# An RWKV block with FP4 feed-forward: small loads packed into one array, the decay's two chunks side by side, levels 0 and 1 in one burst, and the last feed-forward tiles split into two chunk streams

## The chip, the cores and the metric

The kernel runs on one core of a Trainium2 chip. The core has five engines that take their instructions in order, each from its own queue: TensorE (PE, matrix products; PEld is its weight load), VectorE (DVE), ScalarE (ACT), GpSimd (POOL) and SyncE (SP, which here only issues DMAs). The metric is the device time of one execution in microseconds (us). Lower is better.

## The reference

The input `x` is (2, 4096, 256): two sequences of 4096 tokens with 256 channels. Two small networks are joined by modulation with six vectors that come from a condition `c`:

```python
sa, ca, ga, sb, cb, gb = split(silu(c) @ wmod)
h = layernorm(x) * (1 + ca) + sa
x = x + ga * rwkv(h)                      # two layers, then a layernorm
h = layernorm(x) * (1 + cb) + sb
x = x + gb * fp4_linear(silu(fp4_linear(h, w_gate)) * fp4_linear(h, w_up), w_down)
```

A layer of `rwkv` has a time mix and a channel mix. The time mix shifts the sequence by one token, makes five mixtures of `x` and the shift (w, k, v, r, g) through two small products `tm_w1`, `tm_w2`, projects them to r, k, v, g, and makes a decay `w = exp(-exp(time_decay + tanh(wx @ td_w1) @ td_w2))` per token and channel. Four heads of 64 channels then run a recurrence over all 4096 tokens:

```python
out_t  = r_t @ (S + u * k_t v_t^T)
S      = S * w_t + k_t v_t^T
```

`fp4_linear` rounds its input and its weight, in blocks of 16, to the eight magnitudes of a four-bit float and multiplies. The feed-forward is 256 to 704 to 256. All arithmetic is float32.

## The kernel before

A tile is 256 tokens of one sequence, held as two chunks (C = 2) of 128 tokens. There are 2 sequences, 16 tiles each, and 2 layers, so the recurrence `wkv` is run 64 times; I call each run a round. A round does not step token by token. It builds, for each chunk, the 128 by 128 products of queries and keys in seven levels: level `l` holds pairs of tokens that lie in neighbouring halves of a block of `2 * 2**l` tokens. Before each next level DVE multiplies r and k (`upd`) by the decay over the half block, so that level l+1 needs the update of level l. Level 0 reads its own copies `r0`, `k0`, in which ACT has put the bonus `u`, so it does not need the update. The pair products are many small matmuls of 64 rows by 32 columns that write the PSUM tile `pa`. A lock (`head_lock`) lets one round at a time use `pa`, `diag`, `attn` and the state `S`.

The feed-forward (`ffns`) takes a finished tile, normalises it, rounds it to FP4 (`fp4`), transposes it, and then handles chunk 0 and after it chunk 1: gate and up products in two halves, silu on ACT and DVE, `fp4` over 704 columns, six transposes, the down product with `wd`, the residual on POOL. `fp4` is eight DVE instructions and one on ACT, each of which needs the one before.

The order of the work is not written out by hand. The program records its operations through a planner, class `Plan`. Each stream (the first layer of each sequence, the second layer of each sequence, the feed-forward, the feed-forward's weights, the conditioning) is a Python generator that records operations until its queue is full; the planner repeatedly takes the operation that could start first by its own table of durations, and so fixes one static order for each engine. It keeps PSUM banks, work buffers (`slot`, `long`, `tiny`) and estimated ends. All recorded operations therefore carry one line number in the profile, L262, and are told apart by the names of their tiles. Only the loads at the start are recorded directly, at L485; SP issues them in the order in which they stand in its queue, each with a wait on one of eight counters that an earlier load must have raised.

Names that the prediction uses: `slot,td` on PE are the decay's two products (`td1` with 128 rows and 128 columns, `td2` with 64 rows and 128 columns); `pa` the pair products, with `slot,slot` for level 0 (its queries and keys lie in two tiles) and `slot` for the others; `kv` the state's product, 128 rows by 64 columns; `S` and `attn` the products that read the state and the pair matrix; `cWk`, `cWv`, `cWr` the channel mix; `wg`, `wu`, `wd` the feed-forward; `ident` a transpose; `scales` the block scales of `fp4`. In a shape such as `64*32` the profile gives the rows and columns of the array that a matmul uses, which I call its form. A float32 matmul shows as two instructions.

In `td1` the weight is stored twice side by side, so that one matmul over all 256 tokens leaves two copies of its 64 outputs in the 128 partitions; `td2` then takes output half j = 0 from the upper copy and j = 1 from the lower.

Of the kernel before, what the change touches and what calls it, by code (L numbers as in the profile page):

```python
# [37 lines left out]
TINY = 24  # L38
# [3 lines left out]
FFN_SHARE = 1.4  # L42
# [3 lines left out]
MAGIC = 1.5 * 2.0**22  # L46

# [7 lines left out]
    "L0_ffn_w_up", "L0_ffn_w_down", "L0_c", "L0_wmod",  # L55
]
# [47 lines left out]
class Plan:  # L104
# [174 lines left out]

    def run(self, streams, stock):  # L280
        streams = [Stream(*q) for q in streams]
        while True:
# [24 lines left out]
            if not can:  # L307
                assert all(st.gen is None and not st.queue for st in streams), "stuck"
                return
# [72 lines left out]
def rwkv_adaln_fp4_kernel(ctx: ExitStack, tc: tile.TileContext, a: dict, out: bass.AP):  # L382
# [74 lines left out]
    scales = wk.tile([P, 3 * (FI // QB)], F32, name="scales")  # L457
# [32 lines left out]
    with nc.allow_non_contiguous_dma(reason="two vectors of 256"):  # L490
        for b in range(B):
            load(cT[:, :, b], a["L0_c"][b].rearrange("(k p) -> p k", p=P))
# [12 lines left out]
    load(lnw[:1, :D], a["L0_attn_ln_out_w"].unsqueeze(0))  # L505

    def load_mat(name, src, kc):
# [5 lines left out]
    VECS = ["ln1_w", "ln2_w", "x_maa", "w_maa", "k_maa", "v_maa", "r_maa", "g_maa",  # L513
            "gn_w", "gn_b", "ck_maa", "cr_maa", "time_decay", "time_first"]
    lay = []
    for i in range(L):
        w = {}
        vec = const.tile([P, len(VECS), J], F32, name=f"vec{i}")
        for n, v in enumerate(VECS):
            src = a["L0_attn_" + v][i]  # L520
            if v.startswith("time"):
                src = src.rearrange("h k -> (h k)")
            with nc.allow_non_contiguous_dma(reason="a vector of 256"):
                load(vec[:, n, :], src.rearrange("(j p) -> p j", p=P))
            w[v] = vec[:, n, :]

        w1 = a["L0_attn_tm_w1"][i].rearrange("(k p) n -> p k n", p=P)
        w["w1"] = wp.tile([P, J, 8 * E], F32, name=f"w1_{i}")  # L530
        load(w["w1"][:, :, : 5 * E], w1)
        for m in range(5, 8):
            load(w["w1"][:, :, m * E : (m + 1) * E], w1[:, :, 4 * E :])
        w2 = a["L0_attn_tm_w2"][i].rearrange("f e d -> (f e) d")
        w2a = wp.tile([P, D], F32, name=f"w2a_{i}")
        load(w2a, w2[0:P, :])
        w2b = wp.tile([2 * E, D], F32, name=f"w2b_{i}")
        for m in range(2):
            load(w2b[m * E : (m + 1) * E, :], w2[P : 5 * E, :])
        w["w2"] = [w2a[E * f : E * (f + 1), :] for f in range(4)]  # L540
        w["w2b"] = w2b
        for n in ("Wr", "Wk", "Wv", "Wg", "Wo"):
            w[n] = load_mat(f"{n}_{i}", a["L0_attn_" + n][i], J)
        w["wvm"] = const.tile([P, J * H], F32, name=f"wvm{i}")
        w["centred"] = False
        w["td1"] = wp.tile([P, J, 2 * ED], F32, name=f"td1_{i}")
        w["td2"] = wp.tile([2 * ED, D], F32, name=f"td2_{i}")
        for m in range(2):
            load(
                w["td1"][:, :, m * ED : (m + 1) * ED],  # L550
                a["L0_attn_td_w1"][i].rearrange("(k p) n -> p k n", p=P),
            )
            load(w["td2"][m * ED : (m + 1) * ED, :], a["L0_attn_td_w2"][i])
        w["cWk"] = load_mat(f"cWk_{i}", a["L0_attn_cWk"][i], J)
        w["cWv"] = load_mat(f"cWv_{i}", a["L0_attn_cWv"][i], FD // P)
        w["cWr"] = load_mat(f"cWr_{i}", a["L0_attn_cWr"][i], J)
        lay.append(w)
        load_wmod(1 + i)
# [7 lines left out]
    def fp4(nc, src, n, rows, dst, st, y, p):  # L566
# [10 lines left out]

        def blk(t):
            return t[:rows, :n].rearrange("p (b q) -> p b q", q=QB)

        am, sc, inv = (st[:rows, m * (FI // QB) : m * (FI // QB) + nb] for m in range(3))
        sb = src.rearrange("p (b q) -> p b q", q=QB)
        nc.vector.tensor_reduce(am, sb, AX.X, ALU.max, apply_absolute_value=True)
# [4 lines left out]
        nc.vector.scalar_tensor_tensor(blk(y), sb, DOWN, invb, ALU.mult, ALU.mult)  # L588
        nc.vector.tensor_scalar(
            p[:rows, :n].bitcast(I32), y[:rows, :n].bitcast(I32), STEP_BITS, None, ALU.bitwise_and  # L590
        )
        yield
        yv, pv = y[:rows, :n], p[:rows, :n]
        nc.vector.scalar_tensor_tensor(yv, pv, MAGIC, yv, ALU.mult, ALU.add)
        nc.vector.scalar_tensor_tensor(yv, pv, -MAGIC, yv, ALU.mult, ALU.add)
        nc.scalar.activation(yv, yv, AF.Copy, bias=MAGIC)
        yield
        nc.vector.scalar_tensor_tensor(
            dst.rearrange("p (b q) -> p b q", q=QB), blk(y), MAGIC, scb, ALU.subtract, ALU.mult
        )  # L600
# [190 lines left out]
    def wkv(i, b, rk_s, dec_s, v_s):  # L791
# [20 lines left out]
        for l in range(7):  # L812
            h = 1 << l
# [17 lines left out]
            if l == 0:  # L831
                give(r0_s, k0_s)
# [94 lines left out]
    def time_mix(i, b, h):  # L927
# [62 lines left out]
        for k in range(J):  # L990
            mm(pd[:, 0:TT], w["td1"][:, k, :], xw[:, k, :], k == 0, k == J - 1)
        give(xw_s)
        td_s = take_slot()
        td = td_s[:, :TT]
        pl.scalar.activation(td, pd[:, 0:TT], AF.Tanh)
# [14 lines left out]
        for j in range(J):  # L1010
            js = slice(j * ED, (j + 1) * ED)
            mm(os[j][:, :TT], w["td2"][js, j * P : (j + 1) * P], td[js, :], True, True)
# [3 lines left out]
        for j in range(J):  # L1016
            pl.scalar.activation(
                dec[:, :, j, :], os[j][:, :TT].rearrange("p (c t) -> p c t", c=C), AF.Exp,
                bias=w["time_decay"][:, j : j + 1],
            )  # L1020
            pl.close(bks[j])
# [85 lines left out]
    def conditioning():  # L1107
# [5 lines left out]
        lnb_s, wide_s, tmp_s = take_slot(), take_slot(), take_slot()  # L1113
        lnb = lnb_s[:, :D]
# [3 lines left out]
        pl.gpsimd.partition_broadcast(lnb, lnw[:1, :D])  # L1118
# [25 lines left out]
        give(lnb_s, wide_s, tmp_s, lnw)  # L1144
        tiny.append(few)

    def ffn_weights():
# [3 lines left out]
        for src, dst in ((a["L0_ffn_w_gate"], wg), (a["L0_ffn_w_up"], wu)):  # L1151
            for n0 in range(0, FI, P):
                n = min(P, FI - n0)
                wt, y, p = (pl.take(long) for _ in range(3))
                pl.sync.dma_start(out=wt[:n, :D], in_=src[n0 : n0 + n, :])
                yield from fp4(pl, wt[:n, :D], D, n, wt[:n, :D], scales, y, p)
# [9 lines left out]
                long.extend((wt, y, p))  # L1166
                yield
        for m in range(J):
            wt, y, p = (pl.take(long) for _ in range(3))
            pl.sync.dma_start(out=wt[:, :FI], in_=a["L0_ffn_w_down"][m * P : (m + 1) * P, :])  # L1170
            yield from fp4(pl, wt[:, :FI], FI, P, wt[:, :FI], scales, y, p)
# [10 lines left out]
            long.extend((wt, y, p))  # L1182
# [62 lines left out]
    def ffns():  # L1245
        HF = FI // 2
        while "ffn" not in known:
            yield
        for _ in range(B * NT):
            while not done:  # L1250
                yield
# [5 lines left out]
            xf = xn.rearrange("p c d -> p (c d)")  # L1257
            y_s, p_s = pl.take(long), pl.take(long)
            yield from fp4(pl, xf, C * D, P, xf, scales, y_s, p_s)
            long.extend((y_s, p_s))  # L1260
# [5 lines left out]
            give(xn_s)  # L1266
            yield
            ob_s = take_slot()
            ob = v3(ob_s)
            for c in range(C):  # L1270
                cs_ = slice(c * P, (c + 1) * P)
                hb_s = pl.take(long)
                hb = hb_s[:, :FI]
                for s in range(2):
                    fs = slice(s * HF, (s + 1) * HF)
                    bk, gp = pl.bank()
                    for k in range(J):
                        mm(gp[:, :HF], xqT[:, k, cs_], wg[:, k, fs], k == 0, k == J - 1)
                    pl.scalar.activation(hb[:, fs], gp[:, :HF], AF.Sigmoid)
                    pl.vector.tensor_tensor(hb[:, fs], hb[:, fs], gp[:, :HF], ALU.mult)  # L1280
                    pl.close(bk)
                    yield
                    bk, up = pl.bank()
                    for k in range(J):
                        mm(up[:, :HF], xqT[:, k, cs_], wu[:, k, fs], k == 0, k == J - 1)
                    pl.vector.tensor_tensor(hb[:, fs], hb[:, fs], up[:, :HF], ALU.mult)
                    pl.close(bk)
                    yield
                y_s, p_s = pl.take(long), pl.take(long)
                yield from fp4(pl, hb, FI, P, hb, scales, y_s, p_s)  # L1290
                long.extend((y_s, p_s))
                hT_s = pl.take(long)
                hT = hT_s.rearrange("p (f n) -> p f n", f=NF)
                for g in range(2):
                    bk, pt = pl.bank()
                    for f in range(3):
                        at0 = f_at[3 * g + f]
                        tr(pt[:, f * P : (f + 1) * P], hb[:, at0 : at0 + P])
                    pl.scalar.copy(
                        hT[:, 3 * g : 3 * g + 3, :], pt[:, : 3 * P].rearrange("p (f n) -> p f n", f=3)  # L1300
                    )
                    pl.close(bk)
                    yield
                long.append(hb_s)
                bk, y = pl.bank()
                for f in range(NF):
# [39 lines left out]
```

## Time and profile before

| | |
|---|---|
| median of 3 runs | 3216.84 us (3215.44 to 3220.56) |
| the profiled execution | 3216.25 us, its span 3214.5 us |
| granted TensorE clock, mean | 0.970 |
| PE busy | 3034.9 us, 94% of the span |
| DVE busy | 2386.1 us, 74% |
| ACT busy | 1621.0 us, 50% |
| POOL busy | 937.6 us, 29% |

The 1.75 us between span and time lie outside the instructions. The shares are means over three stages that differ: a start in which PE does little, a long middle in which it hardly pauses, and an end in which only the feed-forward is left. A busy PE is counted from the modelled ends of its matmuls, so the start of one group to the start of the next is the better measure of what a group costs.

### The profile page before, as it was taken

The numbers are of one execution on the slowest core, as the hardware profiler recorded it, in microseconds if no ns is written. First come the engines' busy times: TensorE is split into PE (matmuls) and PEld (weight loads), VectorE is DVE, ScalarE is ACT, GpSimd is POOL, SyncE is SP. The second block draws the span as 40 slices with busy tenths as digits, with TensorE's granted clock in tenths as the row PEclk, the third lists the DMA queues.
The fourth block names the chain that finished last, engine by engine and source line by source line (L and its number), as shares of the span: only waits on it lengthen the run. The fifth ranks groups of instructions, "written<-read, shape, count | busy, mean of one in ns | idle before, by whom it ended". The sixth has DMA issues, their size and how long they took to land.

```text
span 3214.5 us, 88104 instructions
## 1 busy us (share of the span) xinstructions
PE 3034.9 (94%) x37948; PEld 2423.3 (75%) x37948; DVE 2386.1 (74%) x6146; ACT 1621.0 (50%) x3244; POOL 937.6 (29%) x857
## 2 busy tenths in 40 slices
PE   3899999999999999999999999999999999999875
PEld 2677778787777778788777777878787787778653
DVE  4687777787877777777777876787787787777764
ACT  1465554555555555555555454555554555554321
POOL 1233332232323333223223232233233233322210
PEclk7899999999999999999999999999999999999987
DMA  4000000000000000000000000000000000000000
GB/s 130 17 20 5 9 8 8 12 15 8 9 8 8 15 9 15 8 6 11 8 15 8 8 11 5 18 5 14 8 9 8 12 11 9 11 2 14 12 4 10
DMA packets 46856, 42.31 MB, mean 13 GB/s; under 512 B 13185, under 2 KB 44930, under 8 KB 46466
## 3 DMA queue, kind: packets, MB, share of 16 engines
q1 hardware_dynamic: 46466, 36.68, 3.8%
q8 instruction: 298, 4.88, 0.6%
q14 instruction: 92, 0.75, 0.1%
HBM read 28.28 MB, written 8.39 MB: 11 GB/s over the span
## 4 chain that ended last, share of the span: by engine, by line
PE 77%; DVE 10%; ACT 6%; issue 3%; POOL 1%; DMA 1%; SPq 1%; POOLq 0%; DVEq 0%; ACTq 0%
PE bank L262 69%; PE pa L262 7%; DVE slot L262 5%; ACT slot L262 3%; DVE long L262 2%; ACT attn L262 2%; DVE tiny L262 1%; PE kv L262 1%; DVE scales L262 1%; POOL slot L262 1%; SPq L485 1%; DVE diag L262 1%; ACT L262 1%; ACT long L262 1%; POOL tiny L262 0%
## 5 line engine op out<-in xcount | busy, mean ns | idle before, releaser
L262 POOL TENSOR_TENSOR slot<-slot,slot 128x512 f32<-128x512 f32 x416 | 503.5, 1224 | 980.0 <-DVE slot L262 692.5
L262 ACT ACTIVATE slot<-bank 128x512 f32<-128x512 f32 (+1 forms) x644 | 338.2, 530 | 692.7 <-PE bank L262 662.1
L262 POOL TENSOR_TENSOR tiny<-tiny,nhalf 128x2 f32<-128x2 f32 (+1 forms) x288 | 291.6, 1015 | 957.5 <-DVE tiny L262 867.3
L262 DVE TENSOR_TENSOR slot<-slot,slot 128x512 f32<-128x512 f32 x512 | 382.7, 749 | 102.4 <-PE pa L262 86.3
L262 PE MATMUL bank<-slot,cWk 128*128 128x256 f32 x1536 | 367.4, 385 | 2.8 <-DVE slot L262 1.7
L262 PE MATMUL bank<-cWv,slot 128*128 128x256 f32 x1536 | 344.1, 380 | 0.0
L262 PEld LDWEIGHTS pa<-slot 64*32 64x32 f32 x19456 | 222.1, 108 | 140.3 <-issue 54.6
L262 PEld LDWEIGHTS bank<-slot,cWk 128*128 128x128 f32 x1536 | 286.4, 191 | 45.7 <-DVE slot L262 2.8
L262 PEld LDWEIGHTS bank<-cWv,slot 128*128 128x128 f32 x1536 | 289.3, 190 | 39.6 <-ACT slot L262 0.3
L262 ACT ACTIVATE slot<-bank,vec 128x256 f32<-128x256 f32 x512 | 233.1, 496 | 154.2 <-PE bank L262 145.7
L262 DVE TENSOR_TENSOR slot<-slot,bank 128x512 f32<-128x512 f32 x192 | 131.0, 682 | 225.8 <-PE bank L262 203.6
L262 PE MATMUL pa<-slot 64*32 64x16 f32 x19456 | 264.2, 190 | 30.4 <-DVE slot L262 10.6
L262 DVE SCALAR_TENSOR_TENSOR slot<-bank,vec,slot 128x256 f32<-128x256 f32 x640 | 273.7, 473 | 18.8 <-PE bank L262 18.2
L262 POOL TENSOR_TENSOR slot<-slot 128x512 f32<-128x512 f32 x128 | 142.1, 1112 | 329.2 <-ACT slot L262 278.4
L262 DVE TENSOR_TENSOR long<-long,bank 128x352 f32<-128x352 f32 x256 | 131.8, 515 | 91.3 <-ACT long L262 67.6
L262 PE MATMUL bank<-ident,slot 128*128 128x128 f32 x1152 | 177.6, 282 | 23.1 <-ACT slot L262 15.9
L262 ACT ACTIVATE slot<-slot,tiny 128x256 f32<-128x256 f32 x256 | 142.1, 594 | 111.8 <-DVE tiny L262 90.3
L262 PE MATMUL bank<-wd,long 128*128 128x256 f32 x768 | 191.6, 402 | 0.2 <-ACT slot L262 0.2
L262 DVE SCALAR_TENSOR_TENSOR slot<-slot,vec,slot 128x256 f32<-128x256 f32 x384 | 179.3, 503 | 12.6 <-POOL slot L262 12.5
L262 ACT ACT_TABLE_LOAD x137 | 175.8, 1283 | 19.2 <-PE bank L262 9.5
L262 ACT COPY slot<-bank 128x512 f32<-128x512 f32 x224 | 130.0, 583 | 103.5 <-PE bank L262 99.5
L262 PE MATMUL bank<-wg,slot 128*128 128x352 f32 x512 | 177.8, 470 | 4.1 <-ACT slot L262 4.1
(112 smaller groups left out, 5796.3 us busy)
## 6 DMA issues: line engine op xcount, KB each, us to landing
slot<-in_L_attn_x_dram SPq DMA_DIRECT2D x64, 256.0 KB, 2.7
out_dram<-slot SPq DMA_DIRECT2D x32, 256.0 KB, 2.2
slot<-in_L_wmod_dram SPq DMA_DIRECT2D x6, 256.0 KB, 6.7
cWk<-in_L_attn_cWk_dram SPq DMA_DIRECT2D x2, 768.0 KB, 5.9
cWv<-in_L_attn_cWv_dram SPq DMA_DIRECT2D x2, 768.0 KB, 6.6
long<-in_L_ffn_w_down_dram SPq DMA_DIRECT2D x2, 352.0 KB, 2.8
long<-in_L_ffn_w_gate_dram SPq DMA_DIRECT2D x5, 128.0 KB, 4.9
long<-in_L_ffn_w_up_dram SPq DMA_DIRECT2D x5, 128.0 KB, 2.0
```

What stands on the lines that cost most here:

```text
L262: fn(*[real(v) for v in a], **{n: real(v) for n, v in k.items()})
L485: nc.sync.dma_start(out=dst, in_=src)
```

## The change

Four things are changed together.

1. **Loads.** Fourteen vectors, `tm_w1` (with its last part repeated), `tm_w2`, `td_w1` and `td_w2` of a layer came by 25 DMAs a layer. They are now laid out ahead of the launch as one array `small` of 128 by 1436, loaded by one DMA a layer; `cT` comes by one instead of two, and `ln_out_w` is loaded to all 128 partitions, where POOL's `partition_broadcast` spread it before.
2. **Decay.** `td_w1` is stored once. Its product is taken by chunk: chunk 0 to partitions 0 to 63, chunk 1 to 64 to 127, each with 128 rows by 64 columns and 128 tokens. `td2` uses row group c for chunk c, four products of 128 tokens for two of 256. The tanh works on 128 columns for 256, the first exponential on four pieces of 128 for two of 256.
3. **Levels 0 and 1** are recorded together, after level 0's update.
4. **Feed-forward.** `fp4` works in place and needs one buffer less, there are three `scales` tiles for one, and the last three tiles (`FFN_TAIL`) go through two streams, one per chunk. Each chunk adds its residual and is stored by itself. The number of `tiny` buffers falls from 24 to 16. A helper `press` lets a stream record more when nothing else can go on.

```diff
-TINY = 24
+TINY = 16
-FFN_SHARE = 1.4
+FFN_TAIL = 3
+FFN_AHEAD = 1
...
-    load(lnw[:1, :D], a["L0_attn_ln_out_w"].unsqueeze(0))
+    load(lnw[:, :D], a["L0_attn_ln_out_w"].unsqueeze(0).to_broadcast([P, D]))
...
-        vec = const.tile([P, len(VECS), J], F32, name=f"vec{i}")
+        small = wp.tile([P, SMALL], F32, name=f"small{i}")
+        load(small, a["small"][i])
...
-        for l in range(7):
-            h = 1 << l
+        def products(l):
...
+        for l in range(7):
+            h = 1 << l
+            for m in {0: (), 1: (0, 1)}.get(l, (l,)):
+                products(m)
-            if l == 0:
+            if l == 1:
                 give(r0_s, k0_s)
...
         for k in range(J):
-            mm(pd[:, 0:TT], w["td1"][:, k, :], xw[:, k, :], k == 0, k == J - 1)
+            for c in range(C):
+                mm(
+                    pd[c * ED : (c + 1) * ED, :P], w["td1"][:, k, :], xw[:, k, c * P : (c + 1) * P],
+                    k == 0, k == J - 1,
+                )
...
         for j in range(J):
-            js = slice(j * ED, (j + 1) * ED)
-            mm(os[j][:, :TT], w["td2"][js, j * P : (j + 1) * P], td[js, :], True, True)
+            for c in range(C):
+                cs_ = slice(c * ED, (c + 1) * ED)
+                js = slice(j * P, (j + 1) * P)
+                mm(os[c][:, js], w["td2"][cs_, js], td[cs_, :], True, True)
...
-        pl.gpsimd.partition_broadcast(lnb, lnw[:1, :D])
...
-    def ffns():
+    ready = [[] for _ in range(C)]
+
+    def ffn_inputs():
...
+            while not done or max(len(q) for q in ready) >= FFN_AHEAD:
...
+            for c in range(C):
+                if n < B * NT - FFN_TAIL:
+                    yield from ffn_chunk(c, b, t, x1_s, xq_s, left)
+                else:
+                    ready[c].append((b, t, x1_s, xq_s, left))
             yield
+    def ffn_chunks(c):
+        for _ in range(FFN_TAIL):
+            while not ready[c]:
+                yield
+            yield from ffn_chunk(c, *ready[c].pop(0))
+
+    def ffn_chunk(c, b, t, x1_s, xq_s, left):
...
+        pl.gpsimd.tensor_tensor(ob, ob, x1[:, c, :], ALU.add)
+        pl.sync.dma_start(out=rows_of(out, b, t)[:, c, :], in_=ob)
...
-        streams += [(ffns(), LATE[2], LEAST[2]), (ffn_weights(), 2.0, 0), (conditioning(), -1.0, 0)]
+        streams += [(ffn_inputs(), LATE[2], LEAST[2]), *((ffn_chunks(c), LATE[2], 1) for c in range(C)), (ffn_weights(), 2.0, 0), (conditioning(), -1.0, 0)]
```

Since the planner makes the order, the order on every engine is drawn anew for the whole run.

## The prediction

> **What bounds the kernel now.** I read the busy shares and the slices first, because they split the run into stages.
>
> ```profile
> PE 3034.9 (94%) x37948; PEld 2423.3 (75%) x37948; DVE 2386.1 (74%) x6146; ACT 1621.0 (50%) x3244; POOL 937.6 (29%) x857
> ...
> PE   3899999999999999999999999999999999999875
> ...
> PEclk7899999999999999999999999999999999999987
> ```
>
> Then the busy time by stretches (PE is the second figure, after the length):
>
> ```profile
> 200.00:3000.00 2800.00, 2751.43 (x35012) 2208.43 (x35008) 2139.04 (x5514) 1492.61 (x2980) 870.73 (x775) 0.99 0.03 10
> 3052.50:3096.80 44.30, 40.32 (x177) 32.81 (x177) 25.75 (x64) 16.90 (x33) 8.91 (x8) 0.92 0.04 12
> 3096.80:3214.50 117.70, 63.21 (x201) 44.24 (x199) 63.13 (x120) 17.53 (x32) 6.40 (x6) 0.76 0.02 7
> 0.00:56.70 56.70, 8.35 (x14) 3.50 (x14) 15.54 (x54) 3.83 (x7) 6.43 (x27) 0.71 0.65 179
> ```
>
> There are three stages with three limits. From 200 to 3000 us PE idles 48.6 of 2800 us: only PE work counts there, and work on DVE, ACT and POOL costs nothing while it stays covered. In the first 57 us PE waits for loads. After 3096.8, where the last channel mix (`cWv`) ends, nothing but feed-forward chunks is left, and PE and DVE are each busy about half the time because they take turns. The timelines show the mechanics. The middle, PE:
>
> ```profile
> 1505.56 1.99 PE L262 MATMUL bank<-slot,Wr 128*128 128x256 f32 x8
> 1507.48 0.73 PE L262 MATMUL pa<-slot 64*32 64x16 f32 x64
> ...
> 1520.36 0.69 PE L262 MATMUL kv<-slot,slot 128*64 128x64 f32 x16
> 1520.97 0.49 PE L262 MATMUL bank<-S,slot 128*128 128x128 f32 x2
> ...
> 1526.57 1.89 PE L262 MATMUL bank<-slot,Wg 128*128 128x256 f32 x8
> 1528.30 1.03 PE L262 MATMUL bank<-slot,td 128*128 128x256 f32 x4
> 1529.16 1.05 PE L262 MATMUL bank<-wu,slot 128*128 128x352 f32 x3
> ```
>
> Read start to start: eight instructions of a full product take 1.73 us before another 128\*128 group (1526.57 to 1528.30), but 1.92 before a group of another form (1505.56 to 1507.48). Leaving the full form costs 0.19 us. `td1` takes 0.86 us; `kv`, in the form that `td1` will have, 0.61 us with its own way out. The start, on POOL and DVE:
>
> ```profile
> 25.23 0.55 POOL L262 PARTITION_BROADCAST slot<-slot  x1 [6.29 <-issue]
> ...
> 34.90 0.73 POOL L262 TENSOR_TENSOR tiny<-tiny,nhalf 128x2 f32<-128x2 f32 x1 [9.12 <-issue]
> ...
> 52.61 0.42 DVE L262 TENSOR_REDUCE scales<-long 128x16 f32<-128x256 f32 x1 [16.79 <-DMA long<-in_L_ffn_w_gate_dram]
> ...
> 56.20 0.87 DVE L262 SCALAR_TENSOR_TENSOR slot<-slot,vec,slot 128x256 f32<-128x256 f32 x2
> ```
>
> The first layer's first mixture (56.20) had its inputs from POOL at 39.9 us, but stands on DVE behind the rounding of the feed-forward's first weight, whose load lands only at 52.6. Last, the end; these two transposes open one chunk's last steps and the next chunk's:
>
> ```profile
> 3185.09 1.54 PE L262 MATMUL bank<-ident,long 128*128 128x128 f32 x6 [7.30 <-DVE long L262]
> ...
> 3186.62 5.14 PE L262 MATMUL bank<-wd,long 128*128 128x256 f32 x12
> ...
> 3203.79 1.54 PE L262 MATMUL bank<-ident,long 128*128 128x128 f32 x6 [7.30 <-DVE long L262]
> ```
>
> One chunk takes 18.7 us, and nothing of the next fills PE's 7.3 us wait.
>
> **The start: -16 us.** SP issues 77 loads before the first of the feed-forward's weights; in the changed kernel's order it issues 28. At about 0.5 us each (a vector's load 0.47) the 77 end at 45.35 us, and in the DMA view by 1.5 us slices the traffic falls to 2 GB/s in the first 9 us and near 30 us, where only vectors move. Without these the bytes decide: 10.1 MB stand up to that weight (two `small` of 0.735 MB, ten square weights, six `wmod` parts and two tiles of x of 0.262, four large ones of 0.786, the rest 0.26). The full slices move 238 to 384 GB/s, mean near 320: 32 us, plus 4 for the first issue and the landing, is 36 against 52.6. The 3.6 us of DVE work from there to the mixture stay. The other chain must not be later: `wmod` and x now queue behind 3.6 MB, so `wmod` lands near 16 for 14.4, and DVE's first statistics are done near 25 for 23.2; but POOL, which waits for issue 6.3 and 9.1 us around the broadcast, answers at once, so the mixture's inputs are there near 31, before DVE is free at 39.5. Bounds by the slices: the load lands between 30 and 46.5 us, a gain of 22 to 6.
>
> **Levels and decay: -15 us.** `td1`: 64 rounds of 0.86 us become 64 of 0.61 (512 columns in half-width pairs, as `kv`'s eight products of 64): -16. If the pairs did not overlap, they would take 0.86 + 0.19 and cost +12, but `kv` speaks against that. The order of the two programs has 1257 and 1323 changes of form on PE, but PE leaves the full form 577 and 589 times, because more of the odd forms now stand side by side: 12 x 0.19 = +2.3. `td2` keeps its columns and gets twice the weight loads: 0, at worst another 0.2 x 64 = +13. Level 0 stood alone in only 9 rounds before; in the others level 1 followed it directly, or other levels stood with it, so one burst saves 9 way outs at about 0.16: -1.4. The burst now starts after DVE's update, and level 1's update waits for 64 products instead of 32, 0.5 us; ACT does four exponentials of 413 ns (the row of 128 columns) for two of 496, 0.66 us. Both lie inside the round: it holds the lock some 27 us (products at 1500.5, last state product 1525) of the 46 us from round to round. Without that cover they would cost 64 x 1.2 = 77 us; the bound from below is 0.
>
> **The Trainium skill on forms.** "TensorEngine Tiling (Array Packing)", Key Properties, says that changing the tiling mode drains the array. If every change cost the 0.19 us, 66 more would make +12.5 instead of +2.3 and the sum 3159; the `kv` row holds its own way out already, which is why I count only exits from the full form.
>
> **The end: -36 us.** The instruction order says what is left after the last product with `attn` (at 3052.5 before). Both kernels still have seven down products then. Before, 162 us follow: 44.3 to the last `cWv`, 117.7 after it. In the changed kernel four chunks instead of five and a half follow the last `cWv`, two tiles with both chunks interleaved. Before it stand 50 us of PE work (two `Wo`, six `cWk`, two each of `cWr` and `cWv`, at 1.73 and 5.2 for a `cWv`: 28; a tile's eight gate and up groups of 1.18: 9.4; three sets of transposes and down products of 3.4: 10; transposes 2). The old kernel lost some 7 of its 44 us to stalls; I take 10: 60. After it, DVE leads: the residual and norm of the last tile 3.8, the two chunks and the last tile's own norm 20.9 (eight products of 0.52, two roundings of 704 columns of 5.6, the rest norms), its rounding 4.3; PE then does the second chunk's transposes (1.5) and down product (4.6): 34. The last tile's transposes, copy and gate and up groups end at 45, its second rounding at 56, transposes and down product 6, `gb` 0.4, POOL 0.7, store 2.7: 66. 60 + 66 = 126 for 162. Bounds: a tenth more stalls (24); or no stalls, and a clock that stays high (49). The stores are 64 of 128 KB for 32 of 256; POOL adds 64 halves for 32 wholes of 1.22; SP and POOL have nothing behind them that PE waits for. `fp4` in place has the same DVE instructions: 0.
>
> **The sum.** The profiled execution took 3216.25, 0.6 below the median. 3216.25 - 16 - 15 - 36 = 3149.
>
> **Rivals.**
> - *Forms cost more:* each change 0.19 and `td2` its 13: 3172. For it: `Wr` before `pa`. Against: `kv`'s row. 0.14.
> - *The end pays half:* two chunks share one DVE, whose 63 us of work in the last 118 do not shrink. 3167. 0.12.
> - *The start gives nothing,* if another load that DVE or PE needs lands late: 3165. 0.06.
> - *Slower:* the new order makes PE wait in the middle, where each engine stops at its first unready instruction, above all PE for ACT's decay. Today PE idles 48.6 us of 2800, 0.76 a round. It needs another 67 us, 1.05 a round, to lose the gain, which is nearly the whole 1.2 us above laid bare. Against it: 19 us of slack a round. From there on over 3216; at 77 exposed 3226. 0.06.
> - *As forecast,* 3128 to 3172 by its own range: 0.62.
>
> The best bounds together (22, 17, 49) give 3128, the worst (6, a loss of 10 with `td1` unpaired, 24) 3196; half of the middle's idle time either way moves each by 24. I give 3115 to 3190. A measurement of this kernel tells about 0.2% (6 us) from no change. Slower holds 0.06, the same 0.02, faster 0.92.
>
> **What would show it.** Start: the `TENSOR_REDUCE` after the first weight at 36 instead of 52.6, no wait for issue on POOL. Decay: a 128\*64 group of 0.61 us. Middle: PE still idle about 49 us of 2800. End: about 126 us after the last `attn` product. A longer PE idle time in the middle, or a mixture that still starts after 50, would make me wrong.

## The result and the profile after

The changed kernel takes 3171.07 us (median of 4 runs, 3167.49 to 3175.74) where the kernel before took 3216.41 (median of 4, 3215.44 to 3220.56) beside it: a ratio of 0.9857, with a 95% interval of 0.9840 to 0.9875. The forecast was 3149, with 3115 to 3190 around it. So the sign and the range hold, and the gain is 45 us where 67 were forecast.

The busy shares, the slices and the granted clock of the changed kernel, from its page:

```profile
PE 3007.1 (95%) x38460; PEld 2406.4 (76%) x38460; DVE 2390.1 (76%) x6146; ACT 1628.4 (51%) x3368; POOL 950.6 (30%) x888
...
PE   5899999999999999999989999999999999999987
...
PEclk8899999999999999999999999999999999999999
```

The first slice went from 3 to 5 and the 7 and the 5 at the end became 8 and 7. Both rims are filled; the middle shows nine tenths as before and has to be read in a finer view. The busy time by stretches (PE second, after the length):

```profile
200.00:3000.00 2800.00, 2719.16 (x35357) 2187.80 (x35356) 2121.01 (x5465) 1488.15 (x3072) 871.05 (x796) 0.99 0.03 10
3046.80:3106.80 60.00, 53.20 (x235) 42.90 (x234) 45.41 (x100) 21.48 (x41) 12.67 (x12) 0.91 0.04 12
3106.80:3165.50 58.70, 39.81 (x145) 27.72 (x143) 40.06 (x80) 12.21 (x23) 4.74 (x6) 0.87 0.03 9
```

From 200 to 3000 us PE now idles 80.8 us of 2800 (2800 - 2719.16) where it idled 48.6. This is what the forecast did not have. After the last `cWv` the run needs 58.7 us for 117.6.

I split both profiled runs at two events: the first layer's first mixture, and the start of the last product with `attn`.

| us | before | after | difference | forecast |
|---|---|---|---|---|
| start to the first mixture | 56.2 | 35.6 | -20.6 | -16 |
| first mixture to the last `attn` product | 2996.2 | 3011.2 | +15.0 | -15 |
| of these, PE busy | 2923.2 | 2907.6 | -15.6 | -15 |
| of these, PE idle | 72.9 | 103.6 | +30.7 | 0 |
| last `attn` product to the end | 162.1 | 118.7 | -43.4 | -36 |
| span | 3214.5 | 3165.5 | -49.0 | -67 |

The start, in the timeline of the changed kernel on POOL and DVE:

```profile
16.80 0.72 POOL L271 TENSOR_TENSOR tiny<-tiny,nhalf 128x2 f32<-128x2 f32 x1 [12.85 <-DVE tiny L271]
21.95 0.70 POOL L271 TENSOR_TENSOR tiny<-tiny,nhalf 128x2 f32<-128x2 f32 x1 [4.44 <-DVE tiny L271]
25.88 1.04 POOL L271 TENSOR_TENSOR slot<-slot 128x512 f32<-128x512 f32 x1 [3.23 <-ACT slot L271]
31.98 0.42 DVE L271 TENSOR_REDUCE scales<-long 128x16 f32<-128x256 f32 x1 [9.14 <-DMA long<-in_L_ffn_w_gate_dram]
35.58 0.88 DVE L271 SCALAR_TENSOR_TENSOR slot<-slot,small,slot 128x256 f32<-128x256 f32 x2
```

The chain is the forecast one: the first feed-forward weight lands, DVE rounds it, and the mixture follows 3.6 us later. POOL no longer waits for issue; it waits for DVE and, ahead of its last step, for ACT. What POOL makes for the mixture is there at 26.9 us where 31 was said.

The end, in PE's timeline of the changed kernel:

```profile
3122.90 1.54 PE L271 MATMUL bank<-ident,long 128*128 128x128 f32 x6 [5.20 <-DVE long L271]
3124.37 4.03 PE L271 MATMUL bank<-wd,long 128*128 128x256 f32 x12
3130.58 0.88 PE L271 MATMUL bank<-ident,long 128*128 128x128 f32 x6 [2.18 <-DVE long L271]
...
3151.27 1.54 PE L271 MATMUL bank<-ident,long 128*128 128x128 f32 x6 [5.88 <-DVE long L271]
...
3157.77 0.82 PE L271 MATMUL bank<-ident,long 128*128 128x128 f32 x6
```

The transposes of a tile's second chunk come 7.7 us after those of its first, then 6.5. Two chunks now cost 28.4 us (3122.90 to 3151.27) where one cost 18.7.

The middle's idle time, from the waits of PE between 200 and 3000 us. Before (us in total, times, longest):

```profile
PE bank L262 <- ACT slot L262: 8.4, 17, 1.1
PE pa L262 <- issue: 6.6, 11, 1.0
PE bank L262 <- DVE slot L262: 6.3, 11, 1.3
PE pa L262 <- DVE slot L262: 4.7, 9, 1.7
PE bank L262 <- POOL slot L262: 4.3, 6, 1.7
```

After:

```profile
PE pa L271 <- DVE slot L271: 13.0, 15, 1.9
PE bank L271 <- ACT slot L271: 12.1, 22, 2.0
PE bank L271 <- POOL slot L271: 10.3, 11, 2.0
PE bank L271 <- DVE slot L271: 9.9, 14, 2.8
PE bank L271 <- DVE long L271: 8.1, 5, 6.6
```

No single wait carries the difference of 32 us. The four kinds of wait for a `slot` in the list after, and the one for DVE's `long`, are each 3.6 to 8.3 us larger than before, and `pa <- issue` is 1.3 us smaller (5.3 us after). Most single waits last a microsecond or less; the longest is one of 6.6 us. This is not what one late operation looks like; I took it for the sign of another order, which the experiments then tested.

### The profile page after: what moved, and what is told of

It is laid out like the page before. It is cut to its first block, busy times and chain, and to the rows that moved or that the text cites. A ratio compares the mean times of both kernels' runs of the same rounds, so it can differ in the third digit from the quotient of the medians.

```text
span 3165.5 us, 89344 instructions
## 1 busy us (share of the span) xinstructions
PE 3007.1 (95%) x38460; PEld 2406.4 (76%) x38460; DVE 2390.1 (76%) x6146; ACT 1628.4 (51%) x3368; POOL 950.6 (30%) x888
## 5 line engine op out<-in xcount | busy, mean ns | idle before, releaser
L271 POOL TENSOR_TENSOR slot<-slot,slot 128x512 f32<-128x512 f32 (+1 forms) x448 | 511.4, 1155 | 874.3 <-DVE slot L271 646.3
L271 ACT ACTIVATE slot<-bank 128x512 f32<-128x512 f32 (+2 forms) x644 | 332.9, 521 | 729.2 <-PE bank L271 688.2
L271 DVE TENSOR_TENSOR slot<-slot,slot 128x512 f32<-128x512 f32 x512 | 375.6, 736 | 119.4 <-PE pa L271 89.3
L271 PE MATMUL bank<-slot,small 32*128 32x256 f32 (+3 forms) x2816 | 407.8, 366 | 9.1 <-DVE slot L271 5.4
L271 PEld LDWEIGHTS bank<-slot,small 32*128 32x128 f32 (+3 forms) x2816 | 272.5, 180 | 104.1 <-issue 44.5
L271 PEld LDWEIGHTS pa<-slot 64*32 64x32 f32 x19456 | 223.1, 109 | 140.2 <-issue 58.7
L271 ACT ACTIVATE slot<-bank,small 128x256 f32<-128x256 f32 (+1 forms) x640 | 252.7, 451 | 132.3 <-PE bank L271 122.5
L271 PEld LDWEIGHTS bank<-cWv,slot 128*128 128x128 f32 x1536 | 289.0, 190 | 39.2 <-issue 0.3
L271 DVE SCALAR_TENSOR_TENSOR slot<-bank,small,slot 128x256 f32<-128x256 f32 x640 | 273.2, 473 | 34.5 <-PE bank L271 33.7
L271 PE MATMUL bank<-ident,slot 128*128 128x128 f32 x1152 | 179.7, 283 | 20.9 <-ACT slot L271 11.5
L271 DVE SCALAR_TENSOR_TENSOR slot<-slot,small,slot 128x256 f32<-128x256 f32 x384 | 185.9, 519 | 13.7 <-POOL slot L271 13.7
L271 ACT ACTIVATE slot<-slot 128x512 f32<-128x512 f32 x288 | 181.8, 633 | 24.8 <-DVE slot L271 19.9
```

The source lines that it names most:

```text
L271: fn(*[real(v) for v in a], **{n: real(v) for n, v in k.items()})
```

## The experiments

Two theories were on record before the first runs. **A:** a part of the change makes PE wait by itself, wherever it stands. **B:** each part saves what it saves, but the planner draws the order of the whole run anew, and the order of the kernel before happened to be better than the new ones.

For every run: the time with its ratio to the kernel before on the same chip, and from its profile the start of the first mixture, the middle (from there to the last `attn` product), PE's idle time from 200 to 3000 us, the down products still to be done after the last `attn` product, and the end from there. "Kept" means that the order of the kernel before is kept.

| run | order | time | ratio (95%) | mixture | middle | idle | downs left | end |
|---|---|---|---|---|---|---|---|---|
| before | | 3216.4 | 1 | 56.2 | 2996.2 | 48.6 | 7 | 162.1 |
| after | new | 3171.1 | 0.9857 (0.9840-0.9875) | 35.6 | 3011.2 | 80.8 | 7 | 118.7 |
| e1 loads | new | 3205.9 | 0.9977 (0.9960-0.9994) | 35.9 | 3029.1 | 62.9 | 7 | 143.7 |
| e2 decay | new | 3227.3 | 1.0043 (1.0029-1.0056) | 56.0 | 3022.0 | 76.5 | 7 | 148.5 |
| e3 levels | new | 3221.5 | 1.0015 (0.9999-1.0032) | 55.5 | 3018.2 | 74.6 | 7 | 150.8 |
| e4 feed-forward | new | 3211.4 | 0.9987 (0.9973-1.0000) | 55.2 | 3011.6 | 73.6 | 9 | 143.8 |
| e5 loads | kept | 3195.6 | 0.9940 (0.9919-0.9960) | 35.5 | 2990.8 | 53.8 | 7 | 162.2 |
| e6 loads, decay | kept | 3186.6 | 0.9914 (0.9889-0.9939) | 35.6 | 2990.5 | 58.0 | 7 | 159.6 |
| e7 loads, decay, tail | kept | 3147.5 | 0.9791 (0.9762-0.9821) | 35.2 | 2995.5 | 56.0 | 7 | 116.5 |
| e8 before | redrawn | 3238.8 | 1.0079 (1.0053-1.0105) | 55.6 | 3052.6 | 89.8 | 6 | 127.6 |
| e9 after | redrawn | 3217.7 | 1.0013 (1.0001-1.0026) | 35.3 | 3071.9 | 100.7 | 6 | 108.7 |
| e10 after | redrawn | 3162.6 | 0.9851 (0.9827-0.9874) | 35.4 | 3017.2 | 75.6 | 7 | 104.8 |
| e11 after, no levels | new | 3150.2 | 0.9807 (0.9785-0.9828) | 35.3 | 2998.6 | 75.1 | 8 | 115.1 |
| e12 e7 with levels | new | 3171.9 | 0.9882 (0.9856-0.9908) | 36.1 | 3023.3 | 79.8 | 7 | 110.2 |

### One part at a time (e1 to e4)

Each is the kernel before with one of the four edits:

```diff
 # e1: the loads
-    load(lnw[:1, :D], a["L0_attn_ln_out_w"].unsqueeze(0))
+    load(lnw[:, :D], a["L0_attn_ln_out_w"].unsqueeze(0).to_broadcast([P, D]))
...
+        load(small, a["small"][i])
 # e2: the decay
-            mm(pd[:, 0:TT], w["td1"][:, k, :], xw[:, k, :], k == 0, k == J - 1)
+            for c in range(C):
+                mm(
+                    pd[c * ED : (c + 1) * ED, :P], w["td1"][:, k, :ED], xw[:, k, c * P : (c + 1) * P],
+                    k == 0, k == J - 1,
+                )
 # e3: the levels
+            for m in {0: (), 1: (0, 1)}.get(l, (l,)):
+                products(m)
 # e4: the feed-forward
+            for c in range(C):
+                if n < B * NT - FFN_TAIL:
+                    yield from ffn_chunk(c, b, t, x1_s, xq_s, left)
+                else:
+                    ready[c].append((b, t, x1_s, xq_s, left))
```

> The kernel before with the loads alone (one small array a layer, cT in one DMA, ln_out_w loaded to all partitions); the decay's first weight is still stored twice. Theory A (what the parts do adds up, and PE's idle time in the middle belongs to one part): the first mixture starts near 36 us instead of 56.2, the middle is as before (48.6 us of PE idle between 200 and 3000 us), time 3216 - 20 = 3196. Theory B (a new plan moves PE's idle time in the middle by itself, by 10 to 30 us either way, whatever the part): the start gains the same 20, but the idle time between 200 and 3000 us is off 48.6 by over 8, and the time is off 3196 by the same amount.

> The kernel before with the decay by chunks alone. Theory A: PE has about 15 us less work (64 groups of 0.61 instead of 0.86), idle time in the middle stays at 48.6 unless the four exponentials or the halves are what makes PE wait; time 3201 if they are not, about 3230 if this part carries all of the 32 us of idle time that the changed kernel has more. Theory B: idle time off 48.6 by over 8 without more waits for ACT's decay than for anything else.

> The kernel before with levels 0 and 1 in one burst alone. Theory A: 3215 if the burst is harmless (only 9 rounds had level 0 alone), up to 3247 if it carries the 32 us, and then PE's waits on pa for DVE's slot (4.7 us before) grow most. Theory B: idle time off 48.6 by over 8, spread over all kinds of waits.

> The kernel before with the feed-forward's part alone (last three tiles in two streams, rounding in place, three scale tiles, 16 tiny buffers). Theory A: the stretch from the last product with attn to the end is 118 us instead of 162, the middle as before, time 3216 - 43 = 3173; about 3200 if this part carries the idle time of the middle. Theory B: the end gains the same 43, the idle time is off 48.6 by over 8.

Their differences from the kernel before (3213.7 on that chip) are -7.8, +13.6, +7.8 and -2.3 us: together +11, where all four at once give -45. Parts that simply added up could not do that. All four idle 62.9 to 76.5 us from 200 to 3000 us where the kernel before idles 48.6, whatever the part touches: even the feed-forward's edit, most of which concerns the last three tiles. And e1 to e3, which run the old feed-forward code with the same seven down products left, have ends of 143.7 to 150.8 us instead of 162.1. So with a new order both the middle and the end move, here in opposite directions. The end of e4 came out at 143.8 us where both theories had 118; nine down products were left there instead of seven.

One of these runs alone would have misled. The decay's 3227 us (e2) is what theory A gave in case the decay's products carry the whole wait (about 3230); e6 below, where the same products stand in the old order, excludes it.

### The parts in the old order (e5 to e7)

To hold the order still, the planner is shown the old operations, and others are issued in their place. For the loads it gets the old landing times; for the decay it books the old products and exponentials, with the old durations:

```diff
+    def instead(self, *calls):
+        self.rec.calls = [(getattr(getattr(self.nc, eng), fn), a, k) for eng, fn, a, k in calls]
...
             mm(pd[:, 0:TT], w["td1"][:, k, :], xw[:, k, :], k == 0, k == J - 1)
+        pl.instead(*(
+            (
+                "tensor", "matmul",
+                (pd[c * ED : (c + 1) * ED, :P], w["td1"][:, k, :], xw[:, k, c * P : (c + 1) * P]),
+                {"start": k == 0, "stop": k == J - 1},
+            )
+            for k in range(J) for c in range(C)
+        ))
```

Every instruction of e5 then stands on PE, DVE and ACT exactly where it stood before; in e6 only the decay's own instructions differ. e7 keeps the order up to the feed-forward's 29th tile and takes the changed kernel's two chunk streams for the last three:

```diff
+            if n >= B * NT - FFN_TAIL:
+                left = []
+                for c in range(C):
+                    ready[c].append((b, t, x1_s, xq_s, left))
+                continue
```

> The kernel before with the loads packed, as in the first run, but the planner is given the old landing times and the old broadcast (planned, not issued), so that the order of instructions on PE, DVE and ACT is that of the kernel before, instruction by instruction. Theory B (a part's own saving is real, and what the first four runs lost in the middle came from the new order that each of them drew): the first mixture starts near 36 us for 56.2, PE idles about 49 us (46 to 55) between 200 and 3000 us, the end after the last attn product is 162 +- 4, and the time is about 3196 (3191 to 3203). Theory A (the part itself costs the middle, whatever the order): the idle time is 60 or more, as in the run with the loads alone, and the time 3203 or more.

> The same with the decay's new products as well, again in the old order: the planner sees the old products and exponentials, and the new ones are issued in their place. Theory B: another 15 to 16 us of PE work less in the middle (64 x 0.25), idle time still 49 to 56 us, end 162 +- 4, time about 3181 (3174 to 3189). Theory A (the half-height forms, or the four exponentials, make PE wait): idle time 63 or more, time 3196 or more, that is nothing gained over the run with the loads alone in the old order, or a loss as where the decay stood alone (+14).

> Loads and decay in the old order up to the feed-forward's 29th tile, and from there on the last three tiles through two chunk streams with the rounding in place, as in the changed kernel. Levels 0 and 1 stay apart. Theory B: the middle as in the run before this one, and the end shorter by what two streams save: some 2.75 tiles are left after the last cWv at 29 us each, 80 for 117.6, so 125 to 140 for 162; time 3150 (3138 to 3164), which beats the changed kernel (3171). Theory A: 3171 or more.

Measured: 3195.6 (expected 3196), 3186.6 (3181) and 3147.5 (3150) beside 3213.0. All three times lie in theory B's ranges. Two details do not: the idle time of e6 is 58.0 us (49 to 56 expected), and the end of e7 takes 116.5 us (125 to 140 expected). The stretch from 200 to 3000 us in e5, and then in e7:

```profile
200.00:3000.00 2800.00, 2746.17 (x35187) 2204.21 (x35185) 2142.22 (x5501) 1493.28 (x2983) 859.12 (x767) 0.99 0.03 10
```

```profile
200.00:3000.00 2800.00, 2743.97 (x35661) 2201.41 (x35659) 2146.49 (x5509) 1500.40 (x3097) 864.83 (x769) 0.99 0.03 10
```

The idle time is 53.8 and 56.0 us, and 58.0 in e6: nearer to the 48.6 of the kernel before than to the 63 to 77 of the same parts in orders of their own. With the order held, the parts add: -17.4 for the loads (e5), -8.9 for the decay (e6 less e5), -39.2 for the tail (e7 less e6), -65.5 in all. That is theory B's reading, and e7 beats the changed kernel: its ratio of 0.9791 (0.9762 to 0.9821) lies wholly below 0.9857 (0.9840 to 0.9875).

By these times the decay paid less than was forecast (8.9 us for 14). The same stretch in PE's timeline, e5:

```profile
1498.38 1.89 PE L278 MATMUL bank<-slot,Wg 128*128 128x256 f32 x8
1500.11 1.03 PE L278 MATMUL bank<-slot,small 128*128 128x256 f32 x4
1500.97 1.35 PE L278 MATMUL bank<-wu,slot 128*128 128x352 f32 x4
1502.16 1.35 PE L278 MATMUL bank<-wg,slot 128*128 128x352 f32 x4
```

and e6:

```profile
1502.56 1.89 PE L278 MATMUL bank<-slot,Wg 128*128 128x256 f32 x8
1504.38 0.66 PE L278 MATMUL bank<-slot,small 128*64 128x128 f32 x8
1504.96 1.45 PE L278 MATMUL bank<-wu,slot 128*128 128x352 f32 x4
1506.25 1.35 PE L278 MATMUL bank<-wg,slot 128*128 128x352 f32 x4
```

Start to start, `td1` (`slot,small`) goes from 0.86 to 0.58 us. But `Wg` ahead of it goes from 1.73 to 1.82 and `wu` behind it from 1.19 to 1.29: of the 0.28 us saved, 0.19 goes to the neighbours where both are in the full form. In e5 that is so in 25 of the 59 rounds after 200 us. In the other 34, `td1` already had a neighbour in another form and paid for the change itself: 0.96 us beside one such neighbour, 1.06 between two.

I lined the two runs up instruction by instruction from 200 us on, with idle time left out. The `td1` groups take 21.3 us less in e6, `td2` takes 0.8 more, and the 82 other instructions that got a neighbour of another form (or lost one) take 7.2 more, spread evenly over the run (0.3 to 0.7 in every 200 us). That is 13.3 us saved in 59 rounds, or some 14 in all 64, which is what the prediction had (16 less 2.3). The remaining 35423 instructions have the same work and the same neighbours in both runs, and still take 7.3 us more in e6, half of that between 200 and 400 us; between 200 and 300 us the granted clock was 0.91 in e6 and 0.97 in e5. So that part is a difference between two profiles and not one that the edit makes. The times say less: the medians differ by 8.9 us, and from the five runs of e5 and the four of e6 the difference lies between 4 and 13 us (95%). Whether the kernel got the whole 14 stays open.

### The same kernels in another order (e8 to e10)

A third theory is named from here on. **C:** recording levels 0 and 1 in one burst, the only part that e5 to e7 leave out, is what makes the changed kernel's PE wait.

Nothing is computed or loaded otherwise; the planner's window, in which a more urgent operation may go ahead of the one that could start first, is changed:

```diff
-SOON = 40.0
+SOON = 44.0
```

> The kernel before, nothing computed or loaded otherwise; only the planner's window in which a later stream's operation may go first is 44 us of its own clock for 40, so that it draws another order. Theory B: the idle time between 200 and 3000 us rises as in the other runs, to 60 to 80 for 48.6, and the time is 3222 to 3245, or with a shorter end as in the first runs 3210 to 3235. Theory A (the order as such is worth nothing, the old one is no better than another): idle time 45 to 54, time 3210 to 3220.

> The changed kernel with nothing but the planner's window set to 44 for 40, so that it draws another order. Theory B (the idle time of the middle is a matter of the order drawn): idle time between 200 and 3000 us anywhere from 55 to 95 for 80.8, the end 14 to 15 us for each chunk that is left after the last cWv, the time 3155 to 3200, and this run and the next differ from 3171 by 6 us or more in at least one. Theory C (the burst of levels 0 and 1 costs the middle by itself): idle time 75 to 90 here and in the next run.

> The same with 36. Theory B: a third value of the idle time, in 55 to 95, and of the time, in 3155 to 3200. Theory C: idle time 75 to 90.

e8 is the kernel before with 44, e9 and e10 are the changed one with 44 and 36. The kernel before goes from 3213.0 to 3238.8, its idle time from 48.6 to 89.8, which is above the 60 to 80 that I expected:

```profile
200.00:3000.00 2800.00, 2710.21 (x34762) 2176.30 (x34762) 2124.28 (x5425) 1454.27 (x2921) 852.99 (x755) 0.99 0.04 10
```

Nothing but the order differs between these two, so the order alone can cost 41 us of idle time. The changed kernel takes 3162.6, 3171.1 or 3217.7 for the same work. In e9 the whole gain is gone, and the range that I had given it (55 to 95 us of idle time, 3155 to 3200) was too narrow. The stretch of e9, and its largest waits there:

```profile
200.00:3000.00 2800.00, 2699.26 (x35083) 2168.10 (x35070) 2090.42 (x5391) 1449.31 (x3013) 853.64 (x778) 0.98 0.03 10
```

```profile
PE bank L271 <- DVE slot L271: 17.1, 23, 2.8
PE kv L271 <- ACT slot L271: 12.7, 15, 2.2
PE bank L271 <- ACT slot L271: 11.2, 18, 1.5
```

Its middle is 75.7 us longer than that of the kernel before (3071.9 - 2996.2), which eats the 20.9 us of its start and the 53.4 of its end. The waits are again many and mostly short. Both kernels with long middles, e8 and e9, have six down products left at the last `attn` product where the others have seven to nine: a chunk more was done in the middle, where PE is full, instead of in the end, where it waits. That is a small part of the longer middle: in e9 PE is busy 16.7 us longer there and idle 59.1 us longer.

### The levels (e11, e12)

e11 is the changed kernel with level 0 recorded before its update again. e12 is e7 with level 0's products issued at level 1's place:

```diff
             if l == 0:
-                give(r0_s, k0_s)
+                first = list(pl.rec.calls)
+                pl.instead()
+            elif l == 1:
+                pl.rec.calls = first + pl.rec.calls
+                pl.need(pl.rec, r0, False)
+                pl.need(pl.rec, k0, False)
+                give(r0_s, k0_s)
```

> The changed kernel with level 0 again before its update, by itself; it draws a new order as well. Theory C: idle time falls to the 54 to 58 of the runs in the old order, time near 3148. Theory B: a value within the spread of the other redrawn kernels, 60 to 90, time 3155 to 3200.

> The run with loads, decay and tail in the old order (3147), with level 0's products issued together with level 1's at the place of level 1. Because its two buffers are now held longer, the planner's order departs from the old one from the 393rd PE row on. Theory C: idle time 75 or more for 56, time 3165 or more because of the burst. Theory B: idle time 60 to 90 because the order is a new one, time 3150 to 3195; so a high value alone speaks for neither, a value under 58 against both.

Without the levels the changed kernel takes 3150.2, and with them e7 goes from 3147.5 to 3171.9. With e3 that is three comparisons, and in all three the burst is on the slower side: +7.8 (e3, whose interval of 0.9999 to 1.0032 includes no change), +21 (3171.1 - 3150.2) and +24.4 us. But each of the three is a new order as well, and orders alone span 3162.6 to 3217.7. e11 also has an idle time of 75.1 us, in theory B's band and not at the 54 to 58 that theory C wanted, although its time is theory C's. The wait in which the burst should show, that of `pa` for DVE's `slot`, doesn't set the runs apart either: between 200 and 3000 us it is 8.8 to 13.8 us in the five kernels with the burst and 4.7 to 15.3 in the nine without, 12.7 of them in e11 beside 13.0 in the changed kernel. So whether the burst costs anything by itself stays open, and with it what part of the changed kernel's 80.8 us, if any, belongs to it. In e12 the burst did not fit into the old order: its two buffers are held until level 1, and with that the planner departs from the old order (from the 393rd PE row on). Buffers of its own for the burst, which might have held the order, were not tried.

## Why the prediction came out as it did

**The range and the sign: right.** The 45 us are made of four terms of the prediction, three near their forecast and one that was set to zero and isn't. With 3171 us the result lies at the far edge of the 3128 to 3172 that were called "as forecast".

**The start, -16: right, a little short.** The first weight's `TENSOR_REDUCE` came at 31.98 where 36 was said, so the load landed 4 us earlier than worked out; why, the runs don't say. (The 10.1 MB are right, but the list behind them names ten square weights where twelve are loaded, and so adds up to 9.6.) The time gained on the chip in the old order is 17.4 us.

**Levels and decay, -15: the decay's saving is there, and that the middle of the profiled run shows just this total is partly an accident.** PE is busy 15.6 us less in the middle of the profiled run. But in the old order e5, where no PE instruction differs, is already 9.8 us less busy there than the kernel before (2913.4 for 2923.2), and e7 7 us more than e6 with the same order on PE up to the tail. Single profiles differ by that much. The groups that the decay touches save some 14 us, the times of e5 and e6 show 8.9 (4 to 13); what the levels gave by themselves (1.4 forecast) no run shows. `td1` went to 0.58 us, where 0.61 was said.

What I read wrongly is the price of a form: I took the 1.92 of a `Wr` group ahead of `pa` against 1.73 as the cost of leaving the full form. In e6, between 200 and 3000 us, a full product of eight instructions, its idle time left out, takes 1.727 us between full ones (median of 171), 1.820 ahead of another form (57 ahead of `64*32`), 1.831 behind one (42 behind `32*128`), and 1.924 between two (124). The 0.19 is the way out and the way in, at 0.09 and 0.10; that `Wr` had an odd form on both sides. The count by exits stays the same, since each way out has its way in. The Trainium skill, "TensorEngine Tiling (Array Packing)", Key Properties, says that every change of the tiling mode drains the array, and the two halves agree with it. A group in an odd form shows no such difference: eight instructions in `32*128` take 1.063 us in e6 whether their neighbours are full or in yet another form. So the measure is not that e6 has 81 changes more than e5 (1338 for 1257), but that it has 19 exits more (596 for 577), which at 0.19 are 3.7 us. The line-up agrees: of the 7.2 us that the neighbours pay in e6, `td1` itself had paid about 3.7 in e5, so that 3.5 are new.

**"Middle: PE still idle about 49 us of 2800": this is the step that failed.** The prediction set the waits of the middle against each other part by part, found 19 us of slack a round, and left the idle time as it was. But for the loads, the decay and the tail the idle time isn't a sum over parts; it belongs to the order (e1 to e8), and the order was drawn anew. It became 80.8 us, +32 of the 2800 (30.7 in the middle as split above), and that is more than the 18 us by which the profiled run missed the forecast: start and end came out 12 us better. What the burst of levels 0 and 1 adds to it is open. The kernel before sits at the good end: its 48.6 is the lowest of all fourteen rows, and every kernel with a new order idles 63 to 101. With the order held, idle time stays at 54 to 58, and loads, decay and tail together give 65.5 us, close to the 67 of the prediction, which counted the levels as 1.4 of them.

**The end, -36: right.** 118.7 us for 126, of which 60.0 to the last `cWv` (60 forecast) and 58.7 after it (66). That the 60 fits to the tenth is luck: it was added up from 50 us of work and 10 of stalls, and the run shows 53.2 busy and 6.8 idle. The 7 us of stalls that I gave the old kernel there were 4.0 (44.3 less 40.32 busy). With seven down products left, the new tail takes 104.8 to 118.7 us in four runs and the old one 143.7 to 162.2 in six, so the gain doesn't hang on one draw of the order. The rival *the end pays half* falls. e4 got only 18 us at its end, with nine down products left in it; but e11 needs 115.1 us for eight, so the count alone doesn't set the end.

**The rivals.** *The start gives nothing* falls with e5. *Forms cost more* falls at its prices: in e6 the forms cost 3 to 4 us net where it had 12.5, and `td2` costs little (45.0 us busy before, 46.7 after) where it had 13. *Slower, because the new order makes PE wait in the middle* got 0.06, with a need of 67 us more idle time. The mechanism is the one at work, at half that size. In e9 it reaches the point: with 59 us more idle and 17 us more busy time in the middle (132.0 for 72.9 idle, 2939.9 for 2923.2 busy) the changed kernel is no faster than the one before. One draw in three did that, so a chance of 0.06 was too low for it.

## What to carry to other kernels

Where a planner or a compiler's scheduler makes the order, an edit has two effects: its own saving, and a new draw of the whole order, which here is worth -9 to +47 us of 3200 and hides any part below that. Measure the parts with the order held, by showing the scheduler the old operations and issuing the new ones in their place, and measure the order by changing one tie-break that computes nothing. The order that one starts from can be a lucky draw, as it was here, where all ten redrawn orders idled more: then forecast that the idle time rises when it is redrawn; and if a part is sound, keep the order and take the part, as e7 does.

## What the runs showed of the hardware

A change of the array's form costs PE twice where a full product meets another form: 0.09 us for the full product ahead and 0.10 for the one behind (1.820 and 1.831 us for 1.727), in the profiles of before, after, e5 and e6 alike. Both show in PE's timeline as a longer step from start to start and not as a wait. I had expected one price of 0.19 at the way out. For a group in an odd form the step is the same beside a full product and beside another odd form (1.063 us in `32*128`).

Two runs with the same PE instructions in the same order (before and e5; e6 and e7 up to the tail) differ by 11 and 8 us in the time that PE's groups take with idle time left out. In both pairs 7 us of this lie in the first 200 us, and there the run with the lower granted clock takes longer: 0.82 in before and 0.91 in e5, 0.87 in e7 and 0.91 in e6, as means over these 200 us.
